# A window-attention kernel: sums over rows of x in place of sums over rows of v, weights turned in 32 by 32 squares, an adding DMA, and a new order of the steps

## The chip, the core and the metric

The kernel runs on one core of a Trainium2 chip. The metric is the device time of one execution in microseconds (us); the runs of the kernel before took 3617.67 to 3625.38 us, with a median of 3624.63 us. Five engines work side by side, each through its own instructions in order: TensorE (PE) multiplies matrices and writes only into PSUM, eight banks of 512 fp32 columns by 128 partitions; VectorE (DVE) and ScalarE (ACT) read PSUM and SBUF; GpSimd (POOL) works on SBUF; SyncE (SP) issues the DMAs. An instruction that has to wait for another engine holds up everything behind it on its own engine.

## What is computed

The input is 16 samples of 256 rows of 128 features. After a layer norm, a state-space branch (two convolutions, a selective scan over 16 states, an output product) gives s, and six layers of window attention with a feed-forward part give g; the result is x + s * silu(g). The part that the change touches is the attention of each layer:

```python
qkv = x @ Wqkv                                  # 128 -> 3 * 1024, 16 heads of 64
q, k, v = split into heads
q = l2norm(q) * qs;  k = l2norm(k) * ksc
q = q * cos * scale + rotate_half(q) * sin * scale
k = k * cos / scale + rotate_half(k) * sin / scale
# windows of 32 rows; a row sees its own window and the one before it
sim  = einsum('bhwie,bhwje->bhwij', bq, look(bk)) * 8, masked
attn = softmax(sim)
out  = einsum('bhwij,bhwje->bhwie', attn, look(bv))
x    = out @ Wo + x                             # 1024 -> 128
x    = ffn(x) + x                               # norm, 128 -> 682, gelu gate, 341 -> 128
```

## The kernel before

All data are fp32. The activations lie turned in SBUF for the whole run, as `xT`: 128 features on the partitions, 16 samples of 257 columns. The attention works in blocks of 128 rows of one sample, two blocks a sample, 32 a layer, 192 in all. One pass of the loop in lines 816 to 840 is one iteration; it takes the steps of the hand-written list `order` (line 759) one after the other, and each step works on the block that lies so many blocks ahead as the list says: `(project, 4, 0)` projects q of block n + 4 while `(attend, 0)` works on block n. So the list is the order of work on every engine at once. In iteration order the life of a block is:

- `project` (L433): two matmuls of 512 columns each for q, for k, and (`values`) for v, into a pair of PSUM banks. An fp32 matmul shows as two MATMUL records.
- `square` on ACT (L444), `rotate` and `rotate2` on DVE (L454, L465): the projection times a cosine table and, with halves swapped, times a sine table; `add` on POOL (L476) sums the two; `lengths` on DVE (L510) sums the squares by head; `guess` (DVE) and `refine` (POOL, L532 to L535, twelve small instructions, three rounds) give one over the root for two blocks at a time; `scale` on POOL (L542) multiplies by it.
- `turn` (L552): eight transposes of 128 by 128 for q and for k; ACT evicts them to `qT` and `kT` (L556).
- `score`: eight bf16 matmuls that lay down the mask (L585), then 64 matmuls of 64 by 32 by 64 (L599). `greatest` and `subtract` on DVE (L612, L622), `soften` on ACT (L631, exp).
- `turn_weights`, `turned_weights`: eight transposes of the weights and their eviction. `attend` (L655): 64 matmuls of the weights with `v2`, the rows of v of two neighbouring windows, with a column of ones that gives the sums of the weights. `divide_last` and `divide` take the quotient (DVE, ACT).
- `turn_out`, `turned_out`: eight transposes of the result and their eviction; `close` (L705), once in two blocks, is the product with Wo, and `residual` (L718) adds it to `xT`.

v reaches `v2` by ACT (L486) and ten DMAs a block (L497, L498, L500), eight for a first block of a sample.

Beside the blocks run three other streams, cut into pieces that the list calls: `feed` (three times an iteration) advances the feed-forward part of a group of four blocks, which therefore takes four iterations; `prepare` and `norms_on` advance the start of the state-space branch; and the steps under `state` (`bring`, `weigh`, `advance`, `decay`, `drive`, `put_out`) advance the scan by one of 16 states an iteration, 20 iterations for a group, eight groups. So the last 30 iterations or so carry no scan.

PSUM is held as three pairs of banks with the tags a, b, c and two single banks; `where` (line 45) says which step uses which pair.

Of the kernel before, what the change touches and what calls it, by code (L numbers as in the profile page):

```python
# [26 lines left out]
VW = DH + 1  # L27
# [3 lines left out]
def tile_kernel(ctx: ExitStack, tc: tile.TileContext, a, out):  # L31
# [10 lines left out]
    psz = ctx.enter_context(tc.tile_pool(name="psz", bufs=2, space=PSUM))  # L42


    where = dict(q="b", k="b", v="c", qT="c", kT="a", s="c", w="b", av="a", o="a", h="cab")

    def pair(name, which):
        return pst.tile([128, 1024], FP, name=name, tag=which)

    def bank(name):  # L50
        return psz.tile([128, G], FP, name=name, tag="z")
# [15 lines left out]
    wqkv_of, wo_of, ffw_of, qks_of, tab_of = {}, {}, {}, {}, {}  # L67

    def load_wqkv(layer, i):
        w = wts.tile([128, H * DH], FP, name="wqkv", bufs=4)  # L70
        nc.sync.dma_start(out=w, in_=a["Wqkv"][layer, :, i * 1024 : (i + 1) * 1024])
        wqkv_of[layer, i] = w
# [12 lines left out]
    load_wqkv(0, 0)  # L85
    load_qks(0)
    load_wqkv(0, 1)
# [9 lines left out]
    taps = p.tile([128, 4, 2 * DM], FP, name="taps", tag="o")  # L97
# [35 lines left out]
    def load_wo(layer):  # L133
        wo = wts.tile([128, NP, DM], FP, name="wo")
        nc.sync.dma_start(out=wo, in_=a["Wo"][layer].rearrange("(c p) m -> p c m", p=128))
        wo_of[layer] = wo
# [38 lines left out]
    def normed(to, xt, mv, rstd):  # L175
        for i in range(4):
            nc.vector.tensor_scalar(  # L177
                to[:, i, :], xt[:, i, :], mv[:, i, 0:1], rstd[:, i : i + 1],
                ALU.subtract, ALU.mult,
            )  # L180
# [9 lines left out]
    def first_norm(g):  # L190

        if len(first_rows) <= g:
            first_rows.append(load_first(g))
        xt = first_rows[g]
        yield
        stats = row_stats(ff, xt)
        yield
        normed(xt, xt, *stats)
        yield
        pt = turned(xt, "pt1")  # L200
        xn_of[g] = far.tile([128, G], FP, name="xn", bufs=NG)
        for hh, o in halves:
            at = xT[hh, 2 * g : 2 * g + 2, o : o + L]
            nc.scalar.copy(at, pt[hh].rearrange("p (s t) -> p s t", s=2))
            nc.sync.dma_start(out=xn_of[g][hh].rearrange("p (s t) -> p s t", s=2), in_=at)
        yield
# [9 lines left out]
    def before_scan(g, to):  # L216
# [7 lines left out]
        for half in range(2):  # L224
            pz = bank("pz")
# [18 lines left out]
        pl = bank("pl")  # L244
# [9 lines left out]
        pd = bank("pd")  # L254
# [56 lines left out]
    def put_out():  # L311
        g, n = now
        if n == NS + 1:
            y = of[g]["y"]
            po = bank("po")
# [7 lines left out]
    def feed_forward(layer, g):  # L323
# [5 lines left out]
        pt = bank("pt1")  # L329
# [5 lines left out]
        pt = pt.rearrange("p (n d) -> p n d", n=4)  # L335
        stats = row_stats(ff, pt)
        yield
        xt = ff.tile([128, 4, DM], FP, name="xt")
        normed(xt, pt, *stats)
        yield  # L340
        yield
        pt = turned(xt, "pt1")
# [9 lines left out]
        for c, (c0, n) in enumerate(CH):  # L352
            ph = pair("ph", where["h"][c])
# [22 lines left out]
        po = bank("po")  # L376
# [17 lines left out]
    def end(g):  # L394
# [9 lines left out]
        pt = bank("pt1")  # L404
# [9 lines left out]

    vts = [const.tile([128, 2, NP, VW], FP, name=f"vt{i}") for i in range(NB)]
    v2s = [const.tile([128, 4, NP * VW], FP, name=f"v2{i}") for i in range(NB)]
    kTs = [const.tile([128, NP, W + L], FP, name=f"kT{i}") for i in range(2)]
    for t in vts:
        nc.gpsimd.memset(t[:, :, :, DH : DH + 1], 1.0)
    for o in (0, 64):  # L420
        nc.gpsimd.memset(v2s[0][o : o + W, 0, :], 0.0)
# [3 lines left out]
    def product(n, i, pq):  # L425

        b = blocks[n]
        layer, s, blk = b["layer"], b["s"], b["blk"]
        wq = wqkv_of[layer, i]
        xb = xT[:, s, blk * 128 : (blk + 1) * 128]  # L430
# [3 lines left out]
        if n % BL == BL - 1 and i < 2 and layer + 1 < DEPTH:  # L434
            load_wqkv(layer + 1, i + 1)
        return pq

    def project(n, i):
        blocks[n]["pq", i] = product(n, i, pair("pq", where["qk"[i] if n >= 3 else "qw"[i]]))
# [34 lines left out]
    def add(n, i):  # L474
        b = blocks[n]
        nc.gpsimd.tensor_tensor(b["qk", i], b["qk", i], b["t2", i], ALU.add)  # L476

    def values(n):
        blocks[n]["pv"] = product(n, 2, pair("pq", where["v"]))

    def hand_out(n):
        b = blocks[n]
        blk, pq = b["blk"], b["pv"]

        vt = vts[blk]
        nc.scalar.copy(  # L486
            vt[:, :, :, 0:DH].rearrange("p r c d -> p c r d"),
            pq.rearrange("p (c r d) -> p c r d", c=NP, r=2),
        )
        vt = vt.rearrange("p r c d -> p r (c d)")  # L490

        v2 = v2s[blk]
        for r in range(2):
            o = r * 64
            if blk:
                before = vts[blk - 1].rearrange("p r c d -> p r (c d)")
                nc.sync.dma_start(out=v2[o : o + W, 0, :], in_=before[96:128, r, :])  # L497
            nc.sync.dma_start(out=v2[o + W : o + 64, 0, :], in_=vt[0:W, r, :])  # L498
            for j in range(1, 4):
                nc.sync.dma_start(  # L500
                    out=v2[o : o + 64, j, :], in_=vt[W * (j - 1) : W * (j + 1), r, :]
                )
# [25 lines left out]
    def refine(n):  # L528
        ss, y = blocks[n]["ss"], blocks[n]["inv"]
        t = p.tile([128, 4 * H], FP, name="t", bufs=2)  # L530
        for _ in range(3):
            nc.gpsimd.tensor_tensor(t, y, y, ALU.mult)  # L532
            nc.gpsimd.tensor_tensor(t, t, ss, ALU.mult)
            nc.gpsimd.tensor_scalar(t, t, -0.5, 1.5, ALU.mult, ALU.add)
            nc.gpsimd.tensor_tensor(y, y, t, ALU.mult)  # L535
# [22 lines left out]
    def turn(n, i):  # L558

        b = blocks[n]  # L560
        b["pt", i] = transposed(b["qk", i], pair("pt", where[("qT", "kT")[i]]))
# [13 lines left out]
    def score(n):  # L575
# [4 lines left out]
        pscore = b["ps"] = pair("pscore", where["s"])  # L580
# [38 lines left out]
    def subtract(n):  # L619
        b = blocks[n]  # L620
        at = b["at"] = p.tile([128, 1024], FP, name="at")
        nc.vector.tensor_tensor(  # L622
            at.rearrange("p (c r k) -> p r c k", c=NP, r=2),
            b["ps"].rearrange("p (r c k) -> p r c k", r=2, c=NP),
            b["top"].unsqueeze(3).to_broadcast([128, 2, NP, 64]),
# [7 lines left out]
    def turn_weights(n):  # L633
        b = blocks[n]
        b["pt", 2] = transposed(b["at"], pair("pt", where["w"]))

    def turned_weights(n):
        b = blocks[n]
        b["aT"] = p.tile([128, NP, 128], FP, name="aT")
        evict(b["aT"], b["pt", 2])  # L640

    def attend(n):

        b = blocks[n]
        aT, v2 = b["aT"], v2s[b["blk"]]

        b["pav"] = pair("pav", where["av"]).rearrange("p (r x) -> p r x", r=2)[:, :, 0 : 7 * VW]
        b["pav"] = b["pav"].rearrange("p r (c d) -> p r c d", c=7)
        b["pav7"] = [bank("pav7") for r in range(2)]
        for c in (7, 0, 1, 2, 3, 4, 5, 6):  # L650
            for j in range(4):
                jj = slice(j * W, (j + 1) * W)
                for r in range(2):
                    rr = slice(r * 64, (r + 1) * 64)
                    nc.tensor.matmul(  # L655
                        b["pav7"][r][jj, 0:VW] if c == 7 else b["pav"][jj, r, c, :],
                        aT[rr, c, jj],
                        v2[rr, j, c * VW : (c + 1) * VW],
                        start=True,
                        stop=True,  # L660
                    )

    def divide_last(n):

        b = blocks[n]
        o = b["o"] = p.tile([128, 1024], FP, name="o")
        o4 = o.rearrange("p (c r d) -> p r c d", c=NP, r=2)
        den = b["den"] = p.tile([128, 2, NP], FP, name="den", bufs=2)
        for r in range(2):
            last = b["pav7"][r]  # L670
            nc.vector.reciprocal(den[:, r, 7:8], last[:, DH : DH + 1])
            nc.scalar.activation(o4[:, r, 7, :], last[:, 0:DH], AF.Copy, scale=den[:, r, 7:8])

    def divide(n):
        b = blocks[n]
        o4 = b["o"].rearrange("p (c r d) -> p r c d", c=NP, r=2)
        den = b["den"]
        nc.vector.reciprocal(den[:, :, 0:7].unsqueeze(3), b["pav"][:, :, :, DH : DH + 1])  # L678
        nc.vector.tensor_tensor(
            o4[:, :, 0:7, :],  # L680
            b["pav"][:, :, :, 0:DH],
            den[:, :, 0:7].unsqueeze(3).to_broadcast([128, 2, 7, DH]),
            ALU.mult,
        )

    def turn_out(n):
        b = blocks[n]
        if b["blk"] == 0:
            b["oT"] = p.tile([128, NP, L], FP, name="oT")
        else:  # L690
            b["oT"] = blocks[n - 1]["oT"]
        b["pt", 3] = transposed(b["o"], pair("pt", where["o"]))

    def turned_out(n):
        b = blocks[n]
        t0 = b["blk"] * 128
        evict(b["oT"][:, :, t0 : t0 + 128], b["pt", 3])

    def close(n):

        b = blocks[n]
        wo = wo_of[b["layer"]]
        pw = b["pw"] = bank("pw")
        for c in range(NP):
            nc.tensor.matmul(  # L705
                pw[:, 0:L],
                wo[:, c, :],
                b["oT"][:, c, :],
                start=(c == 0),
# [225 lines left out]
```

## Time and profile before

| | |
|---|---|
| runs: median (lowest to highest) | 3624.63 us (3617.67 to 3625.38) |
| the profiled execution: its own time | 3635.42 us |
| its span, first to last instruction | 3633.6 us |
| mean granted clock of TensorE | 0.986 |
| first transposition of weights, block 0 | at 68.1 us |
| last transposition of weights, block 191 | at 3592.0 us |
| DMA: bytes moved, mean rate | 305.03 MB, 84 GB/s |

A line of a group reads: source line, engine, operation, result and operands by the names in the program, shape, count; after the first bar the busy time of the group and the mean duration of one in ns; after the second bar the time that the engine sat idle just before these instructions and what ended most of that. The busy time of TensorE is that of pipelined matmuls, whose ends are modelled, so groups overlap a little. From the first to the last of the two transpositions in the table there are 191 blocks, which makes 18.45 us a block.

### The profile page before, as it was taken

What the parts mean: (1) busy time and instruction counts of PE and PEld (TensorE: products, weight loads), DVE (VectorE), ACT (ScalarE), POOL (GpSimd) and SP (SyncE); (2) the same over time, 40 slices, a digit from 0 to 9 for tenths busy, and PEclk for the clock granted to TensorE, in tenths of its full rate; (3) what the DMA queues carried; (4) which work ended last, traced back from release to release, by engine and by line L of the source; (5) the groups of instructions that cost most, each with busy time, mean ns of one, the idle gap of its engine ahead of it and who ended that gap; (6) DMA issues with size and microseconds to landing.
All of it is one profiled execution on the core that took longest, in us unless ns stands there. A gap on an engine that the chain in (4) does not pass through costs nothing.

```text
span 3633.6 us, 139668 instructions
## 1 busy us (share of the span) xinstructions
PE 3369.5 (93%) x62176; PEld 2194.9 (60%) x62176; DVE 2768.4 (76%) x3866; ACT 2003.4 (55%) x2462; POOL 2626.5 (72%) x2442
## 2 busy tenths in 40 slices
PE   6899999999999999999999999999999999999997
PEld 3555665666566656666666656665666666666664
DVE  6788877777688778877877788778877887777773
ACT  3555555555555555555555555555555555555553
POOL 5578767886688668876887688767886887565651
PEclk9999999999999999999999999999999999999998
DMA  3333323332333333323332333233323332222222
GB/s 88 81 93 92 91 73 95 87 92 72 86 91 91 83 87 87 91 76 88 98 92 78 88 89 92 69 98 96 93 72 91 87 100 75 72 66 66 66 71 56
DMA packets 191844, 305.03 MB, mean 84 GB/s; under 512 B 32718, under 2 KB 58636, under 8 KB 191244
## 3 DMA queue, kind: packets, MB, share of 16 engines
q1 hardware_dynamic: 190956, 295.74, 32.2%
q8 instruction: 490, 8.03, 1.0%
q14 instruction: 110, 0.90, 0.1%
q10 hardware_dynamic: 288, 0.36, 0.0%
HBM read 95.37 MB, written 8.91 MB: 29 GB/s over the span
## 4 chain that ended last, share of the span: by engine, by line
PE 68%; DVE 18%; ACT 5%; issue 4%; POOL 2%; DMA 1%; SPq 1%; ACTq 0%; DVEq 0%; POOLq 0%
PE pq L433 22%; PE pt L552 12%; PE pw L705 8%; PE ph L355 7%; PE pscore L599 6%; PE pav L655 5%; DVE t L454 5%; DVE t L465 5%; ACT sq L444 4%; PE po L378 3%; DVE top L612 1%; PE pz L227 1%; PE pscore L585 1%; DVE at L622 1%; DVE xt L177 1%
## 5 line engine op out<-in xcount | busy, mean ns | idle before, releaser
L476 POOL TENSOR_TENSOR t<-t,t 128x1024 f32<-128x1024 f32 x384 | 970.1, 2527 | 423.3 <-DVE den L678 208.3
L433 PE MATMUL pq<-wqkv,xT 128*128 128x512 f32 x2304 | 1144.3, 623 | 56.0 <-DVE den L678 17.4
L444 ACT ACTIVATE sq<-pq 128x1024 f32<-128x1024 f32 x384 | 393.3, 1024 | 764.8 <-PE pq L433 727.3
L542 POOL TENSOR_TENSOR t<-t,y 128x1024 f32<-128x1024 f32 x384 | 729.0, 1918 | 7.5
L433 PEld LDWEIGHTS pq<-wqkv,xT 128*128 128x128 f32 x2304 | 402.5, 192 | 507.9 <-issue 400.1
L454 DVE TENSOR_TENSOR t<-pq,tab 128x1024 f32<-128x1024 f32 x384 | 468.4, 1220 | 296.9 <-ACT sq L444 296.2
L465 DVE TENSOR_TENSOR t<-pq,tab 128x1024 f32<-128x1024 f32 x384 | 466.2, 1214 | 0.0
L510 DVE TENSOR_REDUCE ss<-sq 128x16 f32<-128x1024 f32 x384 | 463.6, 1207 | 2.6
L655 PEld LDWEIGHTS pav<-v,aT 64*32 64x32 f32 x24576 | 302.3, 106 | 260.9 <-issue 209.9
L655 PE MATMUL pav<-v,aT 64*32 64x65 f32 x24576 | 356.7, 228 | 95.2 <-issue 83.4
L552 PE MATMUL pt<-ident,t 128*128 128x128 f32 x3072 | 393.8, 275 | 22.3 <-ACT oT L556 18.5
L552 PEld LDWEIGHTS pt<-ident,t 128*128 128x128 f32 x3072 | 341.8, 142 | 78.8 <-issue 59.3
L556 ACT COPY aT<-pt 128x1024 f32<-128x1024 f32 x192 | 195.1, 1016 | 323.7 <-PE pt L552 323.7
L705 PE MATMUL pw<-oT,wo 128*128 128x256 f32 x1536 | 347.5, 380 | 1.1 <-ACT oT L556 1.1
L599 PE MATMUL pscore<-kT,qT 64*32 64x64 f32 x24576 | 294.6, 228 | 13.0 <-issue 8.5
L705 PEld LDWEIGHTS pw<-oT,wo 128*128 128x128 f32 x1536 | 284.7, 190 | 35.7 <-ACT oT L556 1.3
L599 PEld LDWEIGHTS pscore<-kT,qT 64*32 64x32 f32 x24576 | 260.7, 106 | 61.3 <-issue 47.0
L486 ACT COPY vt<-pq 128x1024 f32<-128x1024 f32 x192 | 195.5, 1018 | 172.0 <-PE pq L433 171.9
L532 POOL TENSOR_TENSOR t<-y 128x64 f32<-128x64 f32 x288 | 84.2, 292 | 256.9 <-DVE y L525 241.8
L355 PE MATMUL ph<-xn,w 128*128 128x512 f32 (+1 forms) x576 | 259.6, 601 | 5.3 <-DVE t L465 4.2
L612 DVE TENSOR_REDUCE top<-pscore 128x16 f32<-128x1024 f32 x192 | 234.7, 1222 | 35.4 <-PE pscore L599 32.1
L718 DVE TENSOR_TENSOR xT<-pw,xT 64x256 f32<-64x256 f32 x192 | 81.0, 422 | 233.6 <-PE pw L705 232.2
(95 smaller groups left out, 4785.9 us busy)
## 6 DMA issues: line engine op xcount, KB each, us to landing
v<-vt SPq DMA_DIRECT2D x1152, 130.0 KB, 2.4
bc<-rows SPq DMA_DIRECT2D x128, 512.0 KB, 5.4
v<-vt SPq DMA_DIRECT2D x576, 65.0 KB, 2.0
wqkv<-in_Wqkv SPq DMA_DIRECT2D x18, 512.0 KB, 3.6
wo<-in_Wo SPq DMA_DIRECT2D x6, 512.0 KB, 5.7
first<-in_x SPq DMA_DIRECT2D x8, 256.0 KB, 4.3
xn<-xT SPq DMA_DIRECT2D x16, 128.0 KB, 3.5
pad<-xn SPq DMA_DIRECT2D x8, 256.0 KB, 3.2
```

The lines of the kernel that those rows point to most:

```text
L355: nc.tensor.matmul(ph[0:n, i * G : (i + 1) * G], w1[:, i * DI + c0 : i * DI + c0 + n], xn, start=True, stop=True,)
L433: nc.tensor.matmul(pq[:, cc], xb, wq[:, cc], start=True, stop=True)
L444: nc.scalar.activation(b["sq", i], b["pq", i], AF.Square)
L454: nc.vector.tensor_tensor(t1.rearrange("p (h d) -> p h d", h=H), b["pq", i].rearrange("p (h d) -> p h d", h=H), table(n, i, 0).unsqueeze(1 ...
L465: nc.vector.tensor_tensor(t2.rearrange("p (h f d) -> p h f d", h=H, f=2), b["pq", i].rearrange("p (h f d) -> p h f d", h=H, f=2)[:, :, ::- ...
L476: nc.gpsimd.tensor_tensor(b["qk", i], b["qk", i], b["t2", i], ALU.add)
L510: nc.vector.tensor_reduce(b["ss"][:, j * H : (j + 1) * H], b["sq", i].rearrange("p (h d) -> p h d", h=H), AX.X, ALU.add,)
L542: nc.gpsimd.tensor_tensor(t3, t3, b["inv"][:, j * H : (j + 1) * H].unsqueeze(2).to_broadcast([128, H, DH]), ALU.mult,)
L552: nc.tensor.transpose(pt[:, cc], of[:, cc], ident)
L599: nc.tensor.matmul(sc4[jj, r, c, :], qT[rr, c, jj], kT[rr, c, k0 : k0 + 64], start=False, stop=True, skip_group_check=True,)
L655: nc.tensor.matmul(b["pav7"][r][jj, 0:VW] if c == 7 else b["pav"][jj, r, c, :], aT[rr, c, jj], v2[rr, j, c * VW : (c + 1) * VW], start=Tru ...
L705: nc.tensor.matmul(pw[:, 0:L], wo[:, c, :], b["oT"][:, c, :], start=(c == 0), stop=(c == NP - 1),)
```

## The change

The weights of the softmax no longer act on rows of v but on rows of x. The product of each head's part of Wv with its part of Wo is one 128 by 128 matrix, computed once a layer (`mix`, two halves of 16 matmuls of 64 by 128 by 128, and two evictions). `attend` then sums rows of x with the weights, for all 16 heads at once: for each of the four windows of a block and each of the two windows seen (f), one matmul with 32 rows of x as weights and 512 columns (16 heads by 32 rows) streaming, eight a block, seven for the first block of a sample. `keep` evicts the result into `z`, and `close` multiplies each head's 128 by 256 part of `z` by its mixed matrix, 16 matmuls for two blocks, half of them at the end of one iteration and half in the next. The projection of v, its DMAs, the transposes of the weights and of the result, and the divisions after `attend` are gone.

The sums of the weights are a reduction on DVE (`sums`), the division a product on POOL (`share`), and the turning is one DVE instruction (`swap`) that transposes every 32 by 32 square. `subtract` lays the weights out for it. `windows` turns 128 rows of x back on TensorE, ACT copies them, and one or two DMAs make the copy that is shifted by a window. `add` is a DMA on POOL's queue that adds t2 to t1. `refine` takes ten small instructions in place of twelve. `normed` moves from DVE to ACT, with two small POOL instructions more; the feed-forward's transposed rows are copied from PSUM by ACT first. All PSUM is one tile with places given by hand, and `order` is new. `Wv` comes turned from the host's layout of the inputs.

```diff
-    where = dict(q="b", k="b", v="c", qT="c", kT="a", s="c", w="b", av="a", o="a", h="cab")
+    where = dict(m="6", z1="2", z2="6", q="4", k="4", qT="0", kT="2", s="0", h0="0", h1="2", h2="4", pw="7", px="3", f="6", n="2")
+    psum = pst.tile([128, 8, G], FP, name="psum")
+    def pair(name):
+        i = int(where[name])
+        return psum[:, i : i + 2, :].rearrange("p b x -> p (b x)")
...
-    def normed(to, xt, mv, rstd):
+    def normed(pool, to, xt, mv, rstd):
+        less = pool.tile([128, 4], FP, name="less", bufs=2)
+        nc.gpsimd.tensor_tensor(less, mv[:, :, 0], rstd, ALU.mult)
+        nc.gpsimd.tensor_scalar(less, less, -1.0, None, ALU.mult)
         for i in range(4):
-            nc.vector.tensor_scalar(
-                to[:, i, :], xt[:, i, :], mv[:, i, 0:1], rstd[:, i : i + 1],
-                ALU.subtract, ALU.mult,
+            nc.scalar.activation(
+                to[:, i, :], xt[:, i, :], AF.Identity,
+                bias=less[:, i : i + 1], scale=rstd[:, i : i + 1],
             )
...
+    def mix(half):
...
+        for i in range(4):
+            for r in range(2):
+                rr, c = slice(r * 64, (r + 1) * 64), 4 * half + i
+                nc.tensor.matmul(pm[:, r, i, :], wvT[rr, c, :], wo[rr, c, :], start=True, stop=True)
+        nc.scalar.copy(mix_of[layer][:, :, 4 * half : 4 * half + 4, :], pm)
...
     def add(n, i):
         b = blocks[n]
-        nc.gpsimd.tensor_tensor(b["qk", i], b["qk", i], b["t2", i], ALU.add)
+        nc.gpsimd.dma_start(out=b["qk", i], in_=b["t2", i], accum_op=ALU.add)
+    def windows(n):
+        b = blocks[n]
+        px = bank("px")
+        nc.tensor.transpose(
+            px[:, 0:DM], xT[:, b["s"], b["blk"] * 128 : (b["blk"] + 1) * 128], ident
+        )
+        xw = b["xw"] = p.tile([128, 2, DM], FP, name="xw", bufs=3)
+        nc.scalar.copy(xw[:, 0, :], px[:, 0:DM])
+        nc.sync.dma_start(out=xw[W:128, 1, :], in_=xw[0 : 128 - W, 0, :])
+        if b["blk"]:
+            nc.sync.dma_start(out=xw[0:W, 1, :], in_=blocks[n - 1]["xw"][128 - W : 128, 0, :])
...
+    def sums(n):
+        b = blocks[n]
+        den = b["den"] = p.tile([128, H], FP, name="den", bufs=2)
+        nc.vector.tensor_reduce(
+            den, b["at"].rearrange("p (f h k) -> p h f k", f=2, h=H), AX.XY, ALU.add
+        )
+        nc.vector.reciprocal(den, den)
+    def share(n):
+        b = blocks[n]
+        at = b["at"].rearrange("p (f h k) -> p f h k", f=2, h=H)
+        nc.gpsimd.tensor_tensor(
+            at, at, b["den"].unsqueeze(1).unsqueeze(3).to_broadcast([128, 2, H, W]), ALU.mult
+        )
+    def swap(n):
+        b = blocks[n]
+        b["aT"] = p.tile([128, 2, H * W], FP, name="aT")
+        nc.vector.transpose(b["aT"].rearrange("p f x -> p (f x)"), b["at"])
     def attend(n):
...
+        b["pz"] = [pair("z1"), pair("z2")]
+        for f in (1, 0):
             for j in range(4):
                 jj = slice(j * W, (j + 1) * W)
+                lone = j == 0 and b["blk"] == 0
+                if f == 0 and lone:
+                    continue
+                nc.tensor.matmul(
+                    b["pz"][j // 2][:, j % 2 * 512 : (j % 2 + 1) * 512],
+                    xw[jj, 1 - f, :],
+                    aT[jj, f, :],
+                    start=(f == 1),
+                    stop=(f == 0 or lone),
+                )
+    def keep(n, i):
...
+        nc.scalar.copy(
+            b["z"][:, :, t0 : t0 + 2 * W].rearrange("p h (j q) -> p j h q", j=2),
+            b["pz"][i].rearrange("p (j h q) -> p j h q", j=2, h=H),
+        )
+    def close(n, half):
...
+        for h in range(8 * half, 8 * half + 8):
             nc.tensor.matmul(
+                b["pw"][:, 0:L], mixed[:, h, :], b["z"][:, h, :],
+                start=(h == 0), stop=(h == H - 1), skip_group_check=True,
             )
```

The new list, as it stands after the change (`close` and `residual` are taken in every second iteration, `guess` and `refine` likewise, as before):

```python
order = (
    (lengths, 3, 1), (share, 0), (prepare, None), (swap, 0), (state, None, drive),
    (feed, None), (project, 4, 0), (square, 4, 0), (norms_on, None), (close, -1, 1),
    (guess, 3), (rotate, 4, 0), (state, None, decay), (rotate2, 4, 0), (feed, None),
    (residual, -1), (score, 1), (state, None, advance), (mix, None, 0), (attend, 0),
    (greatest, 1), (refine, 3), (project, 4, 1), (subtract, 1), (scale, 2, 1),
    (rotate, 4, 1), (rotate2, 4, 1), (keep, 0, 0), (keep, 0, 1), (soften, 1),
    (sums, 1), (turn, 2, 1), (turned_k, 2), (state, None, weigh), (square, 4, 1),
    (lengths, 4, 0), (mix, None, 1), (scale, 2, 0), (close, 0, 0), (state, None, bring),
    (feed, None), (add, 4, 0), (turn, 2, 0), (windows, 1), (add, 4, 1),
    (turned_q, 2), (state, None, put_out),
)
```

In the feed-forward part the pieces between two calls of `feed` are cut anew: of a group's twelve, the fourth holds the transposes and the statistics, the fifth the norm, the sixth the transposes back, the ninth the first product with its gelu, the eleventh the second product with its sum into `xT`.

## The prediction

> **What bounds the kernel now.** I read the busy line first, then the groups, the chain of waits, and the windows of four blocks in mid-run, because a block is the unit that repeats.
>
> ```profile
> PE 3369.5 (93%) x62176; PEld 2194.9 (60%) x62176; DVE 2768.4 (76%) x3866; ACT 2003.4 (55%) x2462; POOL 2626.5 (72%) x2442
> ...
> PE 68%; DVE 18%; ACT 5%; issue 4%; POOL 2%; DMA 1%; SPq 1%; ACTq 0%; DVEq 0%; POOLq 0%
> ...
> L433 PE MATMUL pq<-wqkv,xT 128*128 128x512 f32 x2304 | 1144.3, 623 | 56.0 <-DVE den L678 17.4
> ...
> L476 POOL TENSOR_TENSOR t<-t,t 128x1024 f32<-128x1024 f32 x384 | 970.1, 2527 | 423.3 <-DVE den L678 208.3
> ...
> L542 POOL TENSOR_TENSOR t<-t,y 128x1024 f32<-128x1024 f32 x384 | 729.0, 1918 | 7.5
> ...
> L510 DVE TENSOR_REDUCE ss<-sq 128x16 f32<-128x1024 f32 x384 | 463.6, 1207 | 2.6
> ...
> L655 PE MATMUL pav<-v,aT 64*32 64x65 f32 x24576 | 356.7, 228 | 95.2 <-issue 83.4
> ...
> L705 PE MATMUL pw<-oT,wo 128*128 128x256 f32 x1536 | 347.5, 380 | 1.1 <-ACT oT L556 1.1
> ```
>
> TensorE bounds: 17.5 us busy in 18.45 us of a block (3369.5 / 192 against 191 blocks in 3523.9 us). DVE has 14.4 us a block, POOL 13.7, ACT 10.4. The DVE part of the chain (rotations behind the square) says that PE's rest is waiting for DVE; both matter once PE is lighter.
>
> ```profile
> core 0: us, PE busy (x) PEld busy (x) DVE busy (x) ACT busy (x) POOL busy (x), PEclk, DMA share, GB/s
> 1500.00:1518.45 18.45, 17.42 (x457) 11.27 (x444) 16.96 (x29) 9.71 (x12) 16.21 (x21) 1.00 0.26 70
> ...
> sum 73.80, PE 69.90 PEld 46.17 DVE 60.88 ACT 41.06 POOL 62.81; mean PE 17.47 PEld 11.54 DVE 15.22 ACT 10.27 POOL 15.70
> ```
>
> Where the scan runs, DVE and POOL have 15 us too: little room is left on any of the three.
>
> **What the change takes from PE.** v's projection is a third of L433: 381 us, 2.0 us a block. The transposes of weights and result (16 at 0.13 us) 406 us, 2.1 us. The old `attend`, L655, 357 us, 1.9 us. Together 6.0 us a block.
>
> **What it adds to PE.** `close` goes from 8 to 16 products in two blocks: L705 once more, 347.5 us, 1.8 us a block. `windows` is one transpose, 0.13 us. `mix` is 16 matmuls of 128 columns a layer, 32 records of half an L705 record (0.11 us), 20 us in all. The new `attend` is 16 records (8 matmuls, two records each) of 512 columns with only 32 rows; what they cost depends on overlap.
>
> ```profile
> 1500.06 1.99 PE L433 MATMUL pq<-wqkv,xT 128*128 128x512 f32 x4
> ...
> 1512.30 0.41 PE L585 MATMUL pscore<-mask,ident_h 32*32 32x512 bf16 x8
> ...
> 1512.64 1.49 PE L599 MATMUL pscore<-kT,qT 64*32 64x64 f32 x128
> ...
> 1564.76 3.62 PE L705 MATMUL pw<-oT,wo 128*128 128x256 f32 x16
> ...
> 3565.45 3.78 PE L433 MATMUL pq<-wqkv,xT 128*128 128x512 f32 x4
> ```
>
> Four full records of 512 columns take 1.99 us, so 0.43 us each and 0.26 us until the last has landed. One behind the other, 16 would take 16 x 0.43 + 0.2 = 7.1 us. But L585 puts eight records of 512 columns on different squares of the array into 0.41 us, and L599, fp32 with two records a product, needs 12 ns a record of 64 columns where an eighth of 0.43 us would be 54 ns: at least four run at once, the two records of one product notwithstanding. The four windows of a block lie on four different strips of 32 rows and write four different banks. Bounds: 4 x 0.43 + 0.2 = 1.9 us and 7.1 us; I take 1.9, the nearer row being L599.
> The Trainium skill (TensorE: Matmul & The Clock Gate, Part 3: Packing small matmuls) gives 3.07-fold for four strips of 32 rows at 512 columns. By it `attend` would be an estimated 2.5 us; no run here shows four strips yet.
>
> PE loses 6.0 and gains 1.8 + 0.13 + 0.1 + 1.9 = 3.9 us: 15.4 us a block.
>
> **DVE.** Off: the divisions L679, L678, L671 (298 us, 1.55 us a block) and the norms of L177 (89 us, 0.46). On: `sums`, a reduction of 1024 like L510, 1.21 us, with a reciprocal like L678, 0.23; `swap`, which no row shows: every DVE pass over 1024 fp32 here takes 1.21 to 1.23 us, so 1.22 is the low end, and twice that, 2.44, the high one if a square is filled and then emptied; I take 1.22, as all four forms in the trace do. 14.4 - 2.0 + 2.7 = 15.1; by adding up the rows of the new list I get 15.5 (idle gaps within groups aside). DVE becomes as dense as PE.
>
> **POOL.** Off: L476, 2 x 2.53 = 5.05 us a block, two of the twelve refining instructions (0.3 us each, every second block). On: `share`, a product with a broadcast like L542, 1.92 us; `less`, 2 x 0.3 us in four blocks; two DMA issues. Nothing in the trace is issued by POOL. Bounds for what an issue takes of POOL: nothing, and 2.5 us (the addition that it replaces); I take 0.6 us, the SP's time for one issue (0.53 to 0.6 us). POOL: 13.7 - 5.2 + 2.0 + 1.2 = 11.7 us.
> When the sum lands: rows of 512 KB take 3.6 (weights) to 5.7 us (wo). t2 has two buffers, so `rotate2` of the next iteration needs the landing; the product by `scale` comes two iterations later. In the walk below 7 to 10 us lie between, so I cost it at nothing; a landing at 10 us would hold DVE 2 to 3 us an iteration.
> The Trainium skill (SBUF — State Buffer, Who interferes with whom) speaks against the change here: a DMA issued from GpSimd is starved while VectorE holds the shared port, with an example of 620 ns grown to 3100. By it a landing is an estimated 2.5 us later, which the 7 us would still hide; no run here shows it.
>
> **ACT and SP.** Off ACT: `hand_out`, two evictions, `divide_last`: 683 us, 3.6 us a block. On: two `keep` of 1024 like L556 (2.05), the windows' copy (0.3 by L672's 64 columns), norms and the copy of rows (0.55). 10.4 - 0.7 = 9.7 us: beside other work, but its order counts. SP loses eight or ten DMAs a block and gets one or two.
>
> **The sum is not a maximum but a walk** along the new list, for the four iterations that a feed-forward group takes, each engine in its own order. Row durations: project 1.72 us (+0.26 to land), half a `close` 3.6, score 1.8, attend 1.8 (+0.2), turn 1.05, DVE passes 1.22, ACT passes 1.03, refine 3.7 with its gaps (1500.42 to 1504.84 was 4.4 for twelve); the scan with its share of iterations (2/3: advance 0.89, weigh 1.8, drive 0.85). Start 0 is PE's project q.
> Iteration 1 (even): half a close to 5.3, score to 7.1, attend to 8.9, project k lands 10.95, DVE rotates it until 13.4 and ACT squares it until 14.5, which frees banks 4 and 5 for the next q: 14.55.
> Iteration 2: swap ends at 18.5, then statistics, rotation of q (22.8), subtract (26.1), k (28.5). POOL's rstd and `less` after the statistics end at 22.3, and ACT's norm (to 23.7) stands ahead of `keep`, so keep ends at 25.8, half a close at 29.4, turns at 31.15: next q.
> Iteration 3: as the first to project k (42.1); the three `ph` follow turned_k and square k to 48.0; gelu and the three u end at 49.85, and the last of them frees banks 4 and 5: next q at 49.9.
> Iteration 4: `po` lands 54.4, its two sums into xT end at 57.0 and free bank 6 for attend (to 58.7); project k 60.65, keep 61.05, half a close 65.05, turn 66.1, windows: 66.25.
> So 66.25 us for four blocks. The start of the state-space branch (24 records of 0.43 us a group, 82 us in all) is not in it; half of it in PE's gaps, half on the path, makes 0.2 us a block: 16.6 + 0.2 = 16.8 us.
> Before block 0 lie 68.1 us and from block 191 on 41.6 us; both keep their work: 68.1 + 191 x 16.8 + 41.6 = 3318 us of span. The profiled execution takes 1.8 us around its span and 10.8 us more than the median of the runs (0.3%): 3309. I say **3305 us**, 8.8% below before.
>
> A cost that the walk leaves at nothing: PE has gaps of up to 2.5 us in iteration 2. The last line of the fence shows the price where PE ran thin for some 5 us: 3.78 instead of 1.99 us at a granted clock of 0.50. Once in four blocks that would be 1.8 us, 0.45 us a block, 86 us: inside the range.
>
> **Rivals.** (A) The order packs tighter, only DVE's 15.5 us and the gelu's tail count: 15.9 us a block, 110 + 3037 - 9 = 3138 to, with half of the walk's excess, 3220. For it: PE reached 95% in the windows before. Against: in the walk three engines hand over in turn.
> (B) POOL's issue costs 2.5 us or swap 2.44. The two adds stand ahead of `share` in POOL's order, `share` ahead of `swap`, swap ahead of all of DVE's rotations: it delays iterations 1, 2 and 3 by 1.6 to 2.5 us, 72.6 for four, 18.35 with the branch, 3605. Swap alone: 4 x 1.2 more, 18.0, 3535. Still just faster.
> (C) The slower side: the strips don't overlap in fp32. Attend at 7.1 us is on PE's path in iterations 1, 3 and 4 (5.1 more each) and by half in 2: 83.9 for four, 21.2 a block, 4150 us. It decides from 1.65 us a block more, an attend of some 3.7 us, that is below twofold overlap. L599 speaks against it, but with two strips only.
> (D) The change doesn't do what it says: PSUM is one tile now, and if waits were taken for the whole tile, every engine would wait for every other; adding the engines' rows, over 40 us a block. xT is one tile too, written at L718 and read at L433 for other samples, and no wait of L433 on L718 appears.
>
> **How the numbers follow.** Forecast (3230 to 3450) 0.55, A 0.16, B 0.11 up to 3617, C with partial overlap or a POOL worse than B 0.14, D 0.02, and 0.02 for no change. What can be told from no change is 0.2%, 7 us. Faster 0.82, same 0.02, slower 0.16. The range 3180 to 3600 holds the forecast and most of A and B.
>
> **What would show it.** Attend's group at 1.9 to 2.5 us a block and records overlapping; swap at 1.22 us; DVE at 90% or more, PE about as much; about 16.8 us from one swap to the next; POOL not idle-waited by `share`. Wrong it would be if attend took over 3.7 us, if `swap` waited long for `share`, or if `rotate2` waited for a DMA.

## The result, and the profile after

The changed kernel takes 3790.66 us (median of 4 runs, 3783.39 to 3799.27), the kernel before on the same chip 3625.01 us. The ratio is 1.0462, 95% interval 1.0434 to 1.049: 4.6% slower, where 3305 us and 8.8% faster had been forecast. The profiled span is 3797.5 us.

From the page of the changed kernel: the busy line, the chain that ended last, four groups in the form explained above, and a line of the DMA issues (result and operand, queue, count, KB each, median us from issue to landing).

```profile
PE 3331.4 (88%) x38560; PEld 1996.0 (53%) x38560; DVE 2908.2 (77%) x3450; ACT 1910.4 (50%) x2369; POOL 2383.0 (63%) x2550
...
PE 35%; DVE 29%; POOL 18%; issue 12%; ACT 4%; DMA 1%; SPq 0%; POOLq 0%; ACTq 0%; DVEq 0%
...
L487 POOL DMA_DIRECT2D t<-t x384 | 341.9, 890 | 973.8 <-DVE t L476 358.5
...
L671 PE MATMUL psum<-aT,xw 32*128 32x512 f32 x2880 | 562.8, 702 | 216.9 <-DVE aT L658 123.8
...
L658 DVE STREAM_TRANSPOSE aT<-at 128x1024 f32<-128x1024 f32 x192 | 238.1, 1240 | 370.7 <-POOL at L650 358.1
...
t<-t POOLq DMA_DIRECT2D x384, 512.0 KB, 4.7
```

No engine is busy enough to be the bound any more: PE fell from 93 to 88% of the span, POOL from 72 to 63%, and still the span grew. In the chain POOL went from 2 to 18% and "issue", time that no shown work explains, from 4 to 12%. `swap` (L658) costs 1.24 us as forecast, but DVE stood 370.7 us in front of it, nearly all of it waiting for `share` (L650), which POOL does. From the first swap (70.17 us) to the last (3755.34) it is 19.29 us a block; before, it was 18.45, and the forecast was 16.8.

The timeline shows why `share` is late. One stretch of the changed kernel (start, duration, engine, line, operation; in brackets the idle time before it and what ended that):

```profile
1500.33 1.22 DVE L476 TENSOR_TENSOR t<-psum,tab 128x1024 f32<-128x1024 f32 x1
1501.12 0.93 POOL L487 DMA_DIRECT2D t<-t  x1
...
1502.70 0.25 DVE L645 RECIPROCAL den<-den 128x16 f32<-128x16 f32 x1
...
1506.80 0.87 POOL L487 DMA_DIRECT2D t<-t  x1 [4.74 <-issue]
1507.36 2.25 POOL L650 TENSOR_TENSOR at<-at,den 128x1024 f32<-128x1024 f32 x1
1509.64 1.25 DVE L658 STREAM_TRANSPOSE aT<-at 128x1024 f32<-128x1024 f32 x1 [4.49 <-POOL at L650]
1510.94 1.13 PE L671 MATMUL psum<-aT,xw 32*128 32x512 f32 x6 [1.09 <-DVE aT L658]
...
1513.60 0.85 DVE L710 TENSOR_TENSOR xT<-psum,xT 64x256 f32<-64x256 f32 x2
1514.50 3.77 PE L671 MATMUL psum<-aT,xw 32*128 32x512 f32 x8 [2.43 <-DVE xT L710]
...
1518.21 3.30 PE L450 MATMUL psum<-wqk,xT 128*128 128x512 f32 x4
```

All that the second `add` needs was done at 1501.55, when `rotate2` ended, and all that `share` needs at 1502.95, with the reciprocal. POOL is idle, and yet the second `add` begins at 1506.80: 4.74 us after the first issue ended, put down to "issue", which means that no semaphore explains it. `share` stands behind it in POOL's order, `swap` behind `share`, and behind `swap` in DVE's order comes everything else: the residual (L710), which `attend` needs for its banks. PE then has gaps of 1.09 and 2.43 us in a row, and what follows runs slowly: eight records of `attend` in 3.77 us, where sixteen take 2.0 elsewhere in this trace, and `project` in 3.30 us instead of 1.98.

The windows of the same stretch give the granted clock (the third number from the end):

```profile
core 0: us, PE busy (x) PEld busy (x) DVE busy (x) ACT busy (x) POOL busy (x), PEclk, DMA share, GB/s
1502.65:1520.00 17.35, 13.82 (x172) 7.47 (x173) 10.86 (x15) 5.92 (x8) 11.63 (x16) 0.83 0.33 64
```

It is 0.83 there and 0.929 over the span, where the kernel before had 0.986. These are means: the clock in this trace is either full or half, and it is 0.50 from 1514.07 to 1520.89.

The packets of the adding DMAs tell what POOL waits for. An add is 144 packets; the first starts 1.46 us after the issue begins, and the last ends some 4.4 us after it (medians). Within the 192 pairs of adds of one block, the second issue never begins earlier than 0.58 us after the last packet of the first, and in half of them 0.58 to 0.67 us after it. So POOL issues the second add only when the first has landed. The operand doesn't explain it: counted from the end of `rotate2` or of POOL's own last instruction, whichever is later, the second adds begin 532 us late in all, 2.8 us a block, and 71% of them over 1 us late. The profile calls only 187 us of that "issue". Of the 358.5 us for `rotate2`, 316 are a true wait beside it; the rest bears names like that of L508, whose result the add doesn't read:

```profile
POOL t L487 <- DVE t L476: 358.5, 65, 11.0
...
POOL t L487 <- issue: 187.2, 43, 5.6
...
POOL t L487 <- DVE ss L508: 111.0, 26, 7.8
```

(Engine, result and line that waited, what the wait is put down to, total us, times, longest us.) The program sets `dynamic_dma_scratch_size=512`, read here as 512 bytes a partition of SBUF kept for POOL's DMAs; no run shows the unit. The suspicion was that only one such DMA fits.

### The profile page after: what moved, and what is told of

Its sections match the earlier page's. It is cut to its first block, busy times and chain, and to the rows that moved or that the text cites. A ratio compares the mean times of both kernels' runs of the same rounds, so it can differ in the third digit from the quotient of the medians.

```text
span 3797.5 us, 88594 instructions
## 1 busy us (share of the span) xinstructions
PE 3331.4 (88%) x38560; PEld 1996.0 (53%) x38560; DVE 2908.2 (77%) x3450; ACT 1910.4 (50%) x2369; POOL 2383.0 (63%) x2550
## 4 chain that ended last, share of the span: by engine, by line
PE 35%; DVE 29%; POOL 18%; issue 12%; ACT 4%; DMA 1%; SPq 0%; POOLq 0%; ACTq 0%; DVEq 0%
PE psum L450 10%; PE psum L671 6%; PE psum L700 6%; DVE t L465 5%; DVE t L476 5%; POOL at L650 5%; POOL t L546 4%; DVE aT L658 4%; POOL t L487 3%; PE psum L362 3%; DVE hs L301 3%; PE psum L556 3%; PE psum L603 2%; DVE top L616 2%; POOL y L295 2%
## 5 line engine op out<-in xcount | busy, mean ns | idle before, releaser
L487 POOL DMA_DIRECT2D t<-t x384 | 341.9, 890 | 973.8 <-DVE t L476 358.5
L450 PE MATMUL psum<-wqk,xT 128*128 128x512 f32 x1536 | 860.6, 688 | 78.5 <-DVE t L476 50.2
L688 ACT COPY z<-psum 128x1024 f32<-128x1024 f32 x384 | 372.0, 1010 | 846.6 <-PE psum L671 846.0
L671 PE MATMUL psum<-aT,xw 32*128 32x512 f32 x2880 | 562.8, 702 | 216.9 <-DVE aT L658 123.8
L465 DVE TENSOR_TENSOR t<-psum,tab 128x1024 f32<-128x1024 f32 x384 | 467.2, 1217 | 322.9 <-PE psum L450 234.1
L700 PE MATMUL psum<-z,mix 128*128 128x256 f32 x3072 | 700.5, 381 | 1.3 <-ACT z L688 1.3
L700 PEld LDWEIGHTS psum<-z,mix 128*128 128x128 f32 x3072 | 579.6, 191 | 119.1 <-issue 45.5
L455 ACT ACTIVATE sq<-psum 128x1024 f32<-128x1024 f32 x384 | 393.1, 1024 | 261.0 <-PE psum L450 87.8
L658 DVE STREAM_TRANSPOSE aT<-at 128x1024 f32<-128x1024 f32 x192 | 238.1, 1240 | 370.7 <-POOL at L650 358.1
L556 PEld LDWEIGHTS psum<-ident,t 128*128 128x128 f32 x3072 | 374.3, 148 | 280.4 <-issue 128.6
L556 PE MATMUL psum<-ident,t 128*128 128x128 f32 x3072 | 426.2, 285 | 93.9 <-POOL t L546 71.8
L476 DVE TENSOR_TENSOR t<-psum,tab 128x1024 f32<-128x1024 f32 x384 | 466.1, 1214 | 0.0
L508 DVE TENSOR_REDUCE ss<-sq 128x16 f32<-128x1024 f32 x384 | 443.3, 1183 | 1.2 <-ACT sq L455 1.1
L650 POOL TENSOR_TENSOR at<-at,den 128x1024 f32<-128x1024 f32 x192 | 414.2, 2157 | 21.4 <-DVE den L645 16.6
```

What stands on the lines that cost most here:

```text
L450: nc.tensor.matmul(pq[:, cc], xb, wq[:, cc], start=True, stop=True)
L455: nc.scalar.activation(b["sq", i], b["pq", i], AF.Square)
L465: nc.vector.tensor_tensor(t1.rearrange("p (h d) -> p h d", h=H), b["pq", i].rearrange("p (h d) -> p h d", h=H), table(n, i, 0).unsqueeze(1 ...
L476: nc.vector.tensor_tensor(t2.rearrange("p (h f d) -> p h f d", h=H, f=2), b["pq", i].rearrange("p (h f d) -> p h f d", h=H, f=2)[:, :, ::- ...
L487: nc.gpsimd.dma_start(out=b["qk", i], in_=b["t2", i], accum_op=ALU.add)
L508: nc.vector.tensor_reduce(b["ss"][:, j * H : (j + 1) * H], b["sq", i].rearrange("p (h d) -> p h d", h=H), AX.X, ALU.add,)
```

## The experiments

Three theories were put against each other. R (room): the space for POOL's DMAs holds only one add. O (order): the second add waits for the first whatever the space, so that only its place in the list helps. T (TensorE): the time sits in `attend`'s waits for its banks and in the clock, whatever POOL does.

**More room, three times.** One number differs:

```diff
-    nc = bacc.Bacc("TRN2", target_bir_lowering=False, num_devices=1, dynamic_dma_scratch_size=512)
+    nc = bacc.Bacc("TRN2", target_bir_lowering=False, num_devices=1, dynamic_dma_scratch_size=1536)
```

> The changed kernel with 1536 instead of 512 bytes a partition set aside for the descriptors of POOL's DMAs, nothing else. Theory R (ring): the second adding DMA of an iteration cannot be issued until the first has landed, because the space for descriptors holds one such DMA only; POOL stands for 4 to 5 us in front of `share`, and `swap`, the rotations, the sum into xT and the second half of `attend` follow late. It expects POOL's idle time before the adding DMA to fall from 974 us to below 350, the wait of `swap` for `share` from 358 us to below 150, and 3400 us (3330 to 3480). Rival O (order): two adding DMAs follow one another whatever the space: no change, 3760 to 3820 us. Rival T (TensorE): the wait goes, but the time sits in attend's wait for the sum into xT and in the halved clock behind it: POOL's idle falls as with R, yet the time only to 3650 to 3750 us.

Measured: 3403.98 us (3403.73 to 3405.25), ratio to before 0.9395 (0.9379 to 0.941). The groups and the landing from its page:

```profile
PE 3133.4 (92%) x38560; PEld 1925.6 (57%) x38560; DVE 2905.0 (85%) x3450; ACT 1908.4 (56%) x2369; POOL 2376.0 (70%) x2550
...
L487 POOL DMA_DIRECT2D t<-t x384 | 340.3, 918 | 573.6 <-DVE t L476 478.8
...
L671 PE MATMUL psum<-aT,xw 32*128 32x512 f32 x2880 | 454.5, 631 | 51.1 <-DMA xw<-xw 40.4
...
L658 DVE STREAM_TRANSPOSE aT<-at 128x1024 f32<-128x1024 f32 x192 | 237.5, 1237 | 26.9 <-POOL at L650 26.9
...
t<-t POOLq DMA_DIRECT2D x384, 512.0 KB, 4.9
```

The same adds with nearly the same landing time, and 387 us less. DVE's wait in front of `swap` fell from 370.7 to 26.9 us, TensorE's in front of `attend` from 216.9 to 51.1, and in two thirds of the pairs the second issue begins before the first add's last packet, by up to 3.92 us. Counted as above, no second add begins over 1 us late any more (63 us in all, for 532). The profiled span is 395.6 us shorter: TensorE is idle 198 us less and busy 198 us less. The second half goes with the clock, 0.975 for 0.929: a span of 3797.5 us loses 270 us of full clock at the one, a span of 3401.9 us 85 at the other.

The idle time in front of L487 itself stayed at 573.6 us, more than expected; 478.8 of it is put down to `rotate2`, and `share`, which stands behind it, comes late enough to hold `swap` for 26.9 us only. O and T fall: the space alone brings it, and what TensorE lost, by waiting and by the clock, came from POOL.

**Only just more room.** 576 bytes in place of 512.

> The changed kernel with 576 bytes a partition kept for the descriptors of POOL's DMAs, in place of 512; nothing else differs. Theory R1 (what counts is whether a second adding DMA of 512 KB fits beside the first; the two just fail to fit into 512 bytes): about as with 1536 bytes, 3405 us, 3395 to 3450, TensorE's clock about 0.97, the second issue of an iteration before the last packet of the first, idle time of DVE's `swap` for `share` under 60 us. Theory R2 (room has to be free for a whole second DMA with a margin, or only doubling brings it): as with 512 bytes, 3790 us, 3770 to 3800, the second issue never earlier than 0.5 us after the last packet of the first. Something between would mean that only part of the pairs overlap.

Measured: 3404.05 us (3402.63 to 3406.33), ratio 0.9388 (0.937 to 0.9406): R1, the same as with 1536. Its groups are the same too:

```profile
L487 POOL DMA_DIRECT2D t<-t x384 | 343.3, 924 | 574.8 <-DVE t L476 471.6
...
L658 DVE STREAM_TRANSPOSE aT<-at 128x1024 f32<-128x1024 f32 x192 | 237.3, 1236 | 25.0 <-POOL at L650 25.0
```

So two adds do not fit into 512 bytes and do fit into 576. The Trainium skill (DMA: Bandwidth & Descriptors, Terms) gives a descriptor 16 bytes and says that POOL's DMAs write theirs into rings in SBUF; by that figure the two adds need an estimated 33 to 36 places where 512 bytes have 32, 17 or 18 an add. No run shows the places themselves; the traces show 144 packets an add, which makes 9 for each of 16 DMA engines if they share evenly, and the two sizes.

**The second add after `share`.** With 512 bytes, the second add of a block is moved past `share` into the next iteration:

```diff
+        (add, 3, 1),
...
-        (add, 4, 1),
```

> The changed kernel with the second adding DMA (k) moved behind `share` of the next iteration. Theory R: `share` no longer stands behind the wait, which now lies in front of `drive` and is shorter by the 2 us of `share`; 3550 us (3480 to 3650). Rival O expects the same, this run does not tell R from O. Rival T: 3700 us or more, since the order in front of attend is not what costs.

Measured: 3457.51 us (3454.34 to 3466.04), ratio 0.9545 (0.9525 to 0.9565), lower than R's range began. Two groups of its page:

```profile
L487 POOL DMA_DIRECT2D t<-t x384 | 345.1, 899 | 293.1 <-issue 90.4
...
L658 DVE STREAM_TRANSPOSE aT<-at 128x1024 f32<-128x1024 f32 x192 | 237.4, 1236 | 40.6 <-POOL at L650 40.4
```

The second issue still never comes earlier than 0.58 us after the first add's last packet, and POOL still waits 90.4 us for nothing that shows; but `share` no longer stands behind it, and `swap` waits 40.6 us. It recovers 333 of the 387 us, in two ways that this run doesn't tell apart: the wait is shorter (POOL's idle time before L487 is 293.1 us for 973.8, since the first add lands while `share` works), and `share` is no longer queued behind what is left of it.

**The change without the adding DMA.** `add` is POOL's addition again, everything else as changed:

```diff
-        nc.gpsimd.dma_start(out=b["qk", i], in_=b["t2", i], accum_op=ALU.add)
+        nc.gpsimd.tensor_tensor(b["qk", i], b["qk", i], b["t2", i], ALU.add)
```

> The changed kernel with the addition of the two rotated parts done by POOL again (tensor_tensor, as before the change) in the same place of the order. Theory R: 2 x 2.4 us of POOL in place of 0.9 + 4.8 + 0.9 us, so it is faster than the changed kernel in spite of the fuller POOL: 3650 us (3550 to 3720). Rival T: no faster than 3750 us. Rival O expects the same as R.

Measured: 3642.11 us (3636.48 to 3644.19), ratio 1.0047 (1.0031 to 1.0063). From its page:

```profile
PE 3254.0 (89%) x38560; PEld 1977.6 (54%) x38560; DVE 2911.0 (80%) x3450; ACT 1910.4 (52%) x2369; POOL 2960.0 (81%) x2550
...
L487 POOL TENSOR_TENSOR t<-t,t 128x1024 f32<-128x1024 f32 x384 | 923.5, 2419 | 267.6 <-DVE t L476 263.0
...
L658 DVE STREAM_TRANSPOSE aT<-at 128x1024 f32<-128x1024 f32 x192 | 238.3, 1241 | 281.5 <-POOL at L650 281.3
```

With POOL adding 2 x 2.42 us a block ahead of `share`, `swap` waits 281.5 us, and what TensorE was spared brings nothing. The adding DMA is what makes the rest of the change pay: 238 us to the good where two adds fit, 149 us to the bad where they don't.

**What keeps it at 17.2 us a block.** With room the kernel takes 17.22 us from swap to swap, not 16.8. Four more kernels ask where that is. The first moves the feed-forward's second piece behind `keep` (with 1536 bytes):

```diff
         (rotate2, 4, 0),
-        (feed, None),
...
         (keep, 0, 1),
+        (feed, None),
```

> The changed kernel with 1536 bytes, and the second `feed` of an iteration moved from ahead of the sums into the block's end, behind `keep` of the first half. Nothing is left out. It asks where the 0.43 us a block go by which the kernel with 1536 bytes (17.23 us a block) stays above the forecast of 16.8. Theory N (ACT's norm of the feed-forward, 1.65 us, stands in front of `keep`, and `po` in front of attend's banks, so half a close comes late once or twice in four blocks): 1 to 3 us less in four blocks, 50 to 140 us, 3260 to 3355 us. Theory S (the time is the state-space start's convolutions, 3.6 us of TensorE in some blocks, which lie on the path): no change, 3385 to 3420. A loss (over 3420) would mean that the feed-forward's own chain, an issue of one piece later in each iteration, ends last.

Measured: 3387.28 us (3383.96 to 3399.44), ratio 0.9338 (0.9317 to 0.936): 17 us less. That is in the range of S, though S said no change, and far from the 50 to 140 of N.

The second cuts the output step of the last layer in two, so that its load of s has time:

```diff
+        yield
         sg = sg.rearrange("p s t -> p (s t)")
         nc.vector.tensor_tensor(sg, sg, sT, ALU.mult)
...
+        (finish, None),
```

> The changed kernel with 576 bytes (3404.05 us), and the output step of the last layer cut in two: its two loads and the silu stay at the end of an iteration, and the product with s, the four transposes and the sum come in the next iteration behind `residual`. Nothing is left out. In the trace with 576 bytes TensorE stands 5.4 us in front of each of these transposes because the load of s has just been issued, and the project behind them runs at half the clock (3.62 in place of 1.98 us); six of the eight lie inside the loop. Theory E (this is on the path and is a part of what stays above the forecast): 6 x 5.4 to 6 x 7 = 32 to 42 us less, 3360 to 3375. Rival (the wait stands where another would stand): under 10 us, 3394 to 3410.

What it addresses, in the timeline of the kernel with 576 bytes:

```profile
3159.74 0.54 SPq L405 DMA_DIRECT2D sT<-s  x1
...
3162.84 0.69 DVE L410 TENSOR_TENSOR xn<-xn,sT 128x512 f32<-128x512 f32 x1 [5.05 <-DMA sT<-s]
...
3163.59 1.11 PE L414 MATMUL psum<-ident,xn 128*128 128x128 f32 x4 [5.37 <-DVE xn L410]
...
3164.49 3.62 PE L450 MATMUL psum<-wqk,xT 128*128 128x512 f32 x4
```

A load is issued and waited for at once, with TensorE 5.37 us idle and `project` at half speed behind it. Measured: 3385.75 us (3384.7 to 3390.52), ratio 0.9353 (0.9334 to 0.9371): 18 us less, about half of what E gave and more than the rival allowed. From the swap of block 160 to that of block 184, in the last layer, a block fell from 18.15 to 17.56 us.

The third does `windows` an iteration earlier:

```diff
-        xw = b["xw"] = p.tile([128, 2, DM], FP, name="xw", bufs=3)
+        xw = b["xw"] = p.tile([128, 2, DM], FP, name="xw", bufs=4)
...
-        (windows, 1),
+        (windows, 2),
```

> The changed kernel with 576 bytes, `windows` done for block n + 2 in place of n + 1, with four buffers in place of three, so that the shifted copies by DMA (1.8 to 7.3 us to landing) have an iteration more. Nothing is left out. With 576 bytes TensorE and its weight loads stand 42 to 69 us in all in front of `attend` for that DMA. Theory X (on the path): 35 to 70 us less, 3335 to 3370 us. Rival (PE gets there sooner and waits for `share`, `swap` or the residual in its stead): under 15 us less, 3389 to 3410. Slower than 3410 would mean that the transposition of x in the earlier place waits for a residual.

Measured: 3387.66 us (3386.83 to 3390.95), ratio 0.9358 (0.9336 to 0.9379): 16 us less. That is just beyond what the rival allowed and far from X's 35 to 70, though the wait itself is gone. The waits of the kernel with 576 bytes (engine, result, line, what it waited for, total us, times, longest us) had

```profile
PEld psum L671 <- DMA xw<-xw: 69.3, 33, 3.8
...
PE psum L671 <- DMA xw<-xw: 42.3, 30, 3.0
```

and the earlier `windows` leaves neither line among its hundred largest waits; most of what they showed came back as other waits: TensorE's idle time fell by 11 us in all, from 272 to 261.

The fourth takes three of the four taps out of the convolution that starts the state-space branch:

```diff
-            for k in range(4):
+            for k in (0,):
```

> The changed kernel with 576 bytes, with one of the four taps of the convolution at the start of the state-space branch; the other three are left out. That takes 12 records of 0.43 us a group off TensorE, 5.2 us, 41 us for eight groups, of which seven lie in the loop beside the blocks. The prediction put half of the branch's start on the path. As predicted: 18 to 23 us less, about 3384 (3378 to 3390). Theory S (in blocks with the convolution TensorE has no gap left, so all of it and its knock-on are on the path): 36 to 50 us less, 3354 to 3368. If it lay in gaps: 3396 or more.

Measured: 3380.98 us (3378.81 to 3390.53), ratio 0.9342 (0.932 to 0.9364): 23 us of 41 are on the path, about the half that the prediction had.

**Three moves together.** The feed, the output step and `windows`, on 576 bytes:

> The changed kernel with 576 bytes and three moves together, nothing left out: the second `feed` behind `keep` (which alone, with 1536 bytes, brought 17 us), the output step cut in two, and `windows` an iteration earlier. If E and X hold and add up with it: 17 + 32 to 42 + 35 to 70 less than 3404 us, 3275 to 3320 us. If the gains overlap or move to the next wait: 3320 to 3385 us. It would be the fastest of all kernels here in either case; above 3387 the moves harm each other.

Measured: 3373.33 us (3365.36 to 3376.81), ratio 0.9313 (0.9291 to 0.9334). It is the fastest of all, but 31 us below 3404, not the 17 + 18 + 16 = 51 that the moves bring singly: the gains overlap. From its page:

```profile
PE 3100.9 (92%) x38560; PEld 1903.7 (56%) x38560; DVE 2899.3 (86%) x3450; ACT 1911.1 (57%) x2369; POOL 2396.0 (71%) x2550
...
PE 49%; DVE 27%; POOL 12%; ACT 8%; issue 4%; DMA 0%; SPq 0%; ACTq 0%; POOLq 0%; DVEq 0%
```

DMA is gone from the chain (5% with room alone). TensorE is the busiest engine at 92%, but it holds only 49% of the chain, where it held 68% before the change: VectorE and POOL still hand over to it in turn.

## Why the prediction was wrong

**The step that failed** is the one on POOL: "I take 0.6 us" for an issue, and the landing, of which it says "I cost it at nothing". An issue takes POOL 0.89 us, not much more than that. The landing is 4.7 us, within what was assumed, and no instruction that needs the sum is shown waiting for it, just as the walk had it. But the walk asked only who uses the data. The next add on the same queue waits for the landing as well, and that wait stands ahead of `share`: 2.8 us a block that the sum has at nothing. `swap` waiting long for `share` was one of the prediction's own signs of being wrong. The second issue began 4.71 us on average after the end of the first; with 576 bytes it is 2.44 us, in which POOL mostly waits for `rotate2`. The bound of 0 to 2.5 us for an issue was made from the addition that it replaces; nothing in the trace of before was issued by POOL, so the price of a second one in flight was missing, and the upper end was no bound at all.

The 2.5 us by which the prediction, after the Trainium skill (SBUF — State Buffer, Who interferes with whom), would have delayed the landing don't show: with VectorE 77 and 85% busy it is 4.7 and 4.9 us, and SP's own DMAs of 512 KB for the scan take 4.9 in the same trace. The page doesn't say that they should: the section names `tensor_copy` as what seemed to stall such a DMA, and tensor_tensor and tensor_reduce as what did not, and these two are 72% of VectorE's busy time here. The example of 620 and 3100 ns stands in another section of that page and is for a `tensor_copy`.

**Rival B had the mechanism**, POOL's adds ahead of `share`, `share` ahead of `swap`, `swap` ahead of all of DVE's rotations, and placed it at 3605 us with 2.5 us an issue. It was near in what POOL loses: two issues of 2.5 us in place of 0.6 are 3.8 us a block, and the longer issues (0.6 us) and the wait (2.8 us) come to 3.4. It gave 300 us for that, where the wait alone took 387, about half of them in slower records of TensorE. So it called the result just faster; the prediction argued the slower side with C, and its chances name "a POOL worse than B" beside it. C is wrong: sixteen records of `attend` take 2.0 us where nothing holds them, against 1.9 forecast and 7.1 without overlap, so the four strips do overlap in fp32. The 3.07-fold of the Trainium skill (TensorE: Matmul & The Clock Gate, Part 3: Packing small matmuls) would have made it an estimated 2.5 us; this measurement decides, and is nearer to fourfold. D is wrong too: the single PSUM tile made no engine wait for all others, as 17.2 us a block with room shows.

**The clock** was left at nothing, with "0.45 us a block, 86 us" as its price. It came: 17% of the records of `attend` and 16% of those of `project` took over 1.6 times their median in the changed kernel, with 576 bytes 1.5% and 5.5%. The price was too low: TensorE's records took 198 us more than with room. This followed from POOL's wait and went with it when only the space was changed.

**The other terms.** Swap at 1.24 us (forecast 1.22) and DVE at 15.1 us a block (15.5) held; POOL at 12.4 (11.7) has the longer issues and a `share` of 2.07 us in it, for 1.92. TensorE was sized too low: with room it has 16.3 us a block, not 15.4. `attend` is 2.36 us a block in all, `windows` 0.28 instead of 0.13, since a transposition that stands alone takes 0.27 us where eight in a row take 0.13 each, and the projections that stayed take 4.11 where 3.97 were left.

**The walk itself** came near: with room it is 17.22 us a block for 16.8, and 3404 us lies inside the range that the prediction gave its forecast (3230 to 3450), 3% above its point. The rest is spread: the wait for s in the output step, which the walk did not contain (18 us), the copies for `windows` (16), the feed-forward's place (17), less what these share; the three together brought 31 of the 80 us (0.42 us x 191) that lie between. The remainder is in no run by itself; the heavier TensorE is a candidate that was not tested. The branch's start, by the taps that were taken out, was sized right.

## What to carry to other kernels

A DMA issued by a compute engine is an instruction in that engine's order: ask not only who needs its data and how long an issue takes, but whether the queue has room for the next one, and put nothing that is urgent behind a second issue. When an engine idles and the trace names only "issue" as the reason, compare the start of the instruction with the last packet of the DMA before it; if they move together, the space kept for the queue is the first thing to change. The name beside a wait can mislead: here only 187 of 532 us were called "issue", and the rest bore the names of engines whose results the DMA doesn't read. What a wait costs depends on what is queued behind it: moving one line of the list past `share` brought 333 us, while taking away the waits of 36 us for s and of 42 us for the copies, both in front of TensorE, brought 18 and 16.

## What the runs showed of the hardware

- The space kept for POOL's DMAs works as a threshold: at 512 bytes one adding DMA of 512 KB is in flight, at 576 two, and 1536 bring nothing more (3790.66, 3404.05 and 3403.98 us; no size between was run). At 512 POOL itself stands, with all that is queued behind, until 0.58 us or more after the first add's last packet, and no semaphore shows it.
- An adding DMA of 512 KB from SBUF to SBUF lands 4.7 to 4.9 us after its issue (medians) and costs POOL 0.89 to 0.94 us.
- In the stretch shown, TensorE's gaps of 1.1 and 2.4 us, with 1.1 us of work between, stand just before 6.8 us at a granted clock of 0.50, in which `project` takes 3.30 us for 1.98. No run varied the gaps by themselves.
